# Second layer of a two-layer network on one core: the scan's products in a tile of their own, its inputs between product and sum, its spreads ahead of most decays, and group-norm statistics on ScalarE

## The chip, the cores and the metric

The kernel runs on one NeuronCore of a Trainium2 chip. The metric is the device time of one launch in microseconds. Inputs and outputs are float32, 16 images of 128 channels at 56 x 56 pixels.

## The reference

Layer 0 is a block with a 3x3 depthwise position convolution, windowed attention over the four best windows, a 5x5 depthwise convolution of the values, and an MLP. The change leaves it alone. Layer 1 is what matters here:

```python
y = conv3x3(x) + conv_b                              # 128 -> 128 channels
seq = y.reshape(B * H * W, 8, 16)                    # 8 tokens of 16 values
xz = einsum('nld,ed->nle', seq, in_proj_w); xi, z = split(xz, 2)
xc = silu(causal_conv1d(xi) + conv1d_b)              # 32 inner channels
dt, Bm, Cm = split(einsum('nld,ed->nle', xc, x_proj_w), [1, 17])
dt = softplus(dt * dt_proj_w + dt_proj_b)
a = exp(dt[..., None] * -exp(A_log))                 # decay, 32 x 16 states
b = dt[..., None] * Bm * xc[..., None]               # input
for l in range(8):                                   # the scan
    h = a[l] * h + b[l]
    y[l] = sum(h * Cm[l], axis=-1)
out = ((y + D * xc) * silu(z)) @ out_proj_w.T
x = x + silu(group_norm(out, 4 groups) * gn_w + gn_b)
```

The group norm takes mean and variance over 32 channels and all pixels of an image, so its statistics need every block of an image's output.

## The kernel before

`layer0` writes its result `x1` to HBM image by image; then `layer1` runs. Layer 1 cuts each image into 7 blocks of 448 pixels (`BLK`), and one block with its 8 tokens is a *group*: 16 x 7 = 112 groups. A group has 14 *steps*, k = 0 to 13. Steps 2m and 2m + 1 advance token m + 1, one for each half of the state (`jp`, 896 elements in each of 128 partitions). The main loop (L1284) writes the instructions out step by step and by hand, with work for the next groups between; `_chain` (L149) then pins the order of every engine to the written one. No scheduler moves anything.

In one step the engines do this, all through functions of a few lines:

- VectorE: `advance` (L999 for token 7, L1001 otherwise), the *product* of decay `a` and the state before; `complete` (L1006), the *sum* of product and input (not in steps 12 and 13, whose token 7 needs none: its product is its state); `inject` (L991), the *input* of the step four ahead, a product of the spread `x` in PSUM with the broadcast `bb`. Beside these it has `collect` (L1032, steps 3 and 12), `direct_mul` (L960, twice in step 0) and, in steps 9 and 10 of some groups, `bn_stats` (L1080).
- TensorE: `decay` (L973) for the step two ahead and `spread` (L984) for the step five ahead, each as matmuls on 32 rows; then the step's other matmuls: `gather` (L1019), the convolution of the next image (L184), `inner` (L892: the `xc` of the group after next in step 12, the gate `zs` in step 4), `direct` (L955) and `skip` (L1025) in step 13, and smaller ones.
- ScalarE: `decay_exp` (L976), the exponential of the decay in place in PSUM; then what the step's other matmuls leave to it. In steps 4 and 12 it loads the SiLU table (L146), takes two SiLUs (L893), in some groups an eighth of an earlier image's `normalise` (L1121), and loads the exponential's table again. In step 5 it has `rate_log` (L916, L917).
- GpSimd: `weigh` (L1010) in odd steps, token l = 1 to 7, the state times the broadcast `cb`. Between: `rate_sum` (four instructions, L922 to L925) after steps 6 and 8, `product` (L951) in step 10, `gated` (L1035) in steps 4 and 13, and the `store` addition (L1126) in step 2 of some groups.
- SyncE issues every DMA.

The buffers that matter: `a` has two PSUM tiles and the product is written over the decay in place, so an `a` comes free with the sum; `x` has one PSUM tile, free with the input; the states `h` have four SBUF tiles. State tiles are taken in this order: the input of step 0, 2, 4, 6, 8, 10, the product of token 7 in step 12, the input of step 12. So the input of step 12 takes the tile of token 5, which the weigh of token 5 (the one of step 9) must have read.

The names used below: A(k), I(k), S(k) are product, input and sum of step k on VectorE; w(l) is the weigh of token l on GpSimd; k over 13 means the next group.

Of the kernel before, what the change touches and what calls it, by code (L numbers as in the profile page):

```python
# [10 lines left out]
F32 = mybir.dt.float32  # L11
U32 = mybir.dt.uint32
AF = mybir.ActivationFunctionType
ALU = mybir.AluOpType
# [3 lines left out]
P = 128  # L18
H = W = 56
HW = H * W  # L20
# [3 lines left out]
BLK = 448  # L24
NBLK = HW // BLK
# [770 lines left out]
def layer1(ctx: ExitStack, tc: tile.TileContext, x1, t, out, conv):  # L796
# [15 lines left out]
    nc = tc.nc  # L812
# [3 lines left out]
    cst = ctx.enter_context(tc.tile_pool(name="l1c", bufs=1))  # L816
# [16 lines left out]
    vec = conv.vec  # L833
# [5 lines left out]


    for w, name in ((wx, "b_kx"), (wv, "b_dtw")):
        k = w1.tile(list(w.shape), F32, tag="fold", name=name)
# [6 lines left out]
    eps = cst.tile([P, 1], F32, tag="eps1", name="eps1")  # L849
    nc.vector.memset(eps, GN_EPS)  # L850
    neg = cst.tile([P, 1], F32, tag="neg", name="neg")
    nc.vector.memset(neg, -1.0)

    y, tails = conv.y, conv.tails
# [100 lines left out]
        nc.tensor.matmul(pq[0][:, 0:BLK], lhsT=cbm, rhs=p["cb"], start=True, stop=True)  # L955

    def direct_mul(p):
        ud = p["ud"] = w2.tile([P, 2, BLK], F32, tag="ud", name=f"ud_{p['n']}")
        for h in range(2):
            nc.vector.scalar_tensor_tensor(  # L960
                ud[:, h, :], pq[0][:, 0:BLK], vec[:, 6 + h : 7 + h], p["dtx"][:, h, :], ALU.mult, ALU.mult
            )


# [10 lines left out]
    def decay_exp(p, l, jp):  # L975
        nc.scalar.activation(p["a", l, jp], p["a", l, jp], AF.Exp)  # L976
# [16 lines left out]
    def advance(p, l, jp):  # L993

        a, before = p["a", l, jp], p["h", l - 1][:, own(jp), :]
        if l == 7:
            if jp == 0:
                p["h", l] = w4.tile([P, 4, BLK], F32, tag="h", name=f"h_{p['n']}_{l}")
            nc.vector.tensor_mul(p["h", l][:, own(jp), :], a, before)  # L999
        else:  # L1000
            nc.vector.tensor_mul(a, a, before)  # L1001

    def complete(p, l, jp):
        if l < 7:
            h = p["h", l][:, own(jp), :]
            nc.vector.tensor_add(h, p["a", l, jp], h)  # L1006

    def weigh(p, l):
        c = p["c", l] = w4.tile([P, 4, BLK], F32, tag="cst", name=f"cst_{p['n']}_{l}")
# [19 lines left out]
    def collect(p, h):  # L1029
        if h == 0:  # L1030
            p["ym"] = w1.tile([P, 2, BLK], F32, tag="ym", name=f"ym_{p['n']}")
        nc.vector.tensor_add(p["ym"][:, h, :], pq[1][:, 0:BLK], p["ud"][:, h, :])  # L1032

    def gated(p, h):
        nc.gpsimd.tensor_mul(p["ym"][:, h, :], p["ym"][:, h, :], p["zs"][:, h, :])  # L1035
# [1 line left out]
    xrs = {}  # L1037
# [32 lines left out]
    norms = {}  # L1070

    def statistics(b, i):
        if i == 0:
            norms[b] = (
                w2.tile([P, NBLK, 6], F32, tag="stats", name=f"stats_{b}"),
                w2.tile([P, 2], F32, tag="mv", name=f"mv_{b}"),
                w2.tile([P, 6], F32, tag="gst", name=f"gst_{b}"),
            )
        stats, mv, gst = norms[b]
        nc.vector.bn_stats(stats[:, i, :], xrs[b][:, i * BLK : (i + 1) * BLK])  # L1080
        if i == NBLK - 1:
            nc.vector.bn_aggr(mv, stats)

    def group_mean(b, bank):
        stats, mv, gst = norms[b]
        nc.tensor.matmul(pq[bank][:, 0:1], lhsT=gmask, rhs=mv[:, 0:1], start=True, stop=True)
        nc.scalar.copy(gst[:, 0:1], pq[bank][:, 0:1])

    def deviation(b):
        stats, mv, gst = norms[b]  # L1090
        nc.gpsimd.tensor_sub(gst[:, 1:2], mv[:, 0:1], gst[:, 0:1])
        nc.gpsimd.tensor_mul(gst[:, 1:2], gst[:, 1:2], gst[:, 1:2])
        nc.gpsimd.tensor_add(gst[:, 1:2], gst[:, 1:2], mv[:, 1:2])

    def group_var(b, bank):
        stats, mv, gst = norms[b]
        nc.tensor.matmul(pq[bank][:, 0:1], lhsT=gmask, rhs=gst[:, 1:2], start=True, stop=True)
        nc.scalar.activation(gst[:, 2:3], pq[bank][:, 0:1], AF.Ln, bias=eps)
        nc.scalar.activation(gst[:, 3:4], gst[:, 2:3], AF.Exp, scale=-0.5)

    def affine(b):
        stats, mv, gst = norms[b]
        nc.gpsimd.tensor_mul(gst[:, 4:5], gst[:, 3:4], gn_w)
        nc.gpsimd.tensor_mul(gst[:, 5:6], gst[:, 0:1], gst[:, 4:5])
        nc.gpsimd.tensor_sub(gst[:, 5:6], gn_b, gst[:, 5:6])
# [11 lines left out]
            nc.sync.dma_start(res[64:P, half - 64 : half], x1[b][64:P, 0:64])  # L1117

    def normalise(b, k):
        gst, xr = norms[b][2], xrs[b][:, k * half // 4 : (k + 1) * half // 4]  # L1120
        nc.scalar.activation(xr, xr, AF.Silu, bias=gst[:, 5:6], scale=gst[:, 4:5])  # L1121

    def store(b, k, q):
# [8 lines left out]

    def finish(b):

        gst = norms[b][2]
        _act_set(tc, SILU)
        for k in range(2):
            out, res = xrs[b][:, k * half : (k + 1) * half], norms[b, k]
            for q in range(2):
                part = slice(q * half // 2, (q + 1) * half // 2)  # L1140
                nc.scalar.activation(out[:, part], out[:, part], AF.Silu, bias=gst[:, 5:6], scale=gst[:, 4:5])
                nc.vector.tensor_add(res[:, part], res[:, part], out[:, part])
            at = k * half
            nc.sync.dma_start(outv[b, 0, :, at : at + half], res[0:64])
            if k == 0:
                nc.sync.dma_start(outv[b, 1, :, 64 : half + 64], res[64:P])
            else:
                nc.sync.dma_start(outv[b, 1, :, half + 64 : HW], res[64:P, 0 : half - 64])
                nc.sync.dma_start(outv[b, 1, :, 0:64], res[64:P, half - 64 : half])
# [3 lines left out]
    def work(i, k):  # L1153
# [8 lines left out]
        if prev:  # L1162
            if k == 0:
                pe += [partial(gather, prev, 5), partial(gather, prev, 6)]
            if k == 1:
                pe.append(partial(gather, prev, 7))
            if k == 3:
                dve.append(partial(collect, prev, 1))
            if k == 4:
                pool.append(partial(gated, prev, 1))  # L1170
            if k in (5, 6):
                pe.append(partial(project_out, prev, k - 5))
            b = prev["b"]
            if prev["g"] % 2 and k in (9, 10):
                dve.append(partial(statistics, b, prev["g"] - 10 + k))
            if prev["g"] == NBLK - 1:
                if k == 9:
                    dve.append(partial(statistics, b, NBLK - 1))
                if k == 12 and b < NB - 1:
                    residual(b, 0)  # L1180
        two = at(i - 2)
# [102 lines left out]
    for i in range(-2, len(groups) + 3):  # L1284
        for k in range(14):
# [64 lines left out]
```

## Time and profile before

| | |
|---|---|
| median of 3 runs | 8306.25 us (8298.19 to 8308.66) |
| profiled execution, its own time | 8305.77 us |
| its span | 8304.0 us |
| first product of layer 1 / last | 3198.2 us / 8275.8 us from the span's start |
| mean time from one group to the next | 45.35 us |
| busy in the stretch 3400 to 8000 us (of 4600) | PE 4499.84, DVE 4473.50, POOL 4189.50, ACT 3103.93 us |
| granted TensorE clock in that stretch | 0.99 |

Layer 1 takes some 5,080 us of the span. The busy time of VectorE there is 97% of the stretch; a busy share is an average, and it doesn't say which wait ends last in a group. A DVE or POOL instruction's start and duration are in the timeline view, in us; the bracket after it is how long its engine sat idle before it and what ended that. Successive VectorE instructions overlap by some 0.09 us when nothing is waited for, so what counts below is the distance from start to start, called a *slot*.

### The profile page before, as it was taken

The page shows a single profiled execution, that of the slowest core. Times are in us where ns is not written, and L with a number is a line of the kernel's source. Part 1 is how long each engine was busy: PE and PEld are TensorE (multiplying, and loading weights), DVE is VectorE, ACT ScalarE, POOL GpSimd, SP SyncE. Part 2 cuts the span into 40 slices and gives each one's busy share as a digit, 9 for nine tenths or more (in the row PEclk, how much of TensorE's full clock was granted, in tenths as well). Part 3 has the DMA queues.
Part 4 walks back from the last instruction along what each step waited for, and adds up shares of the span by engine and source line. Part 5 has one row for each costly group of instructions (what it writes and reads, how often), then busy time and mean ns, then how long its engine had stood idle before and what let it go on. Part 6 is the DMA issues. An engine that isn't in the chain of part 4 may idle for free.

```text
span 8304.0 us, 151471 instructions
## 1 busy us (share of the span) xinstructions
PE 7835.1 (94%) x52860; PEld 3329.9 (40%) x52860; DVE 7736.9 (93%) x10346; ACT 5642.6 (68%) x10579; POOL 7054.9 (85%) x5692
## 2 busy tenths in 40 slices
PE   5999999999999998999999999999999999999998
PEld 3444444444444453333333333333333333333332
DVE  7999999999999976999999999999999999999998
ACT  4777777777777755666666666666666666666665
POOL 7888788888888725899989999999999989999997
PEclk8999999999999999999999999999999999999998
DMA  3333333333333323333333334334333343334333
GB/s 65 87 86 87 85 89 87 87 87 87 87 87 87 81 79 82 87 93 102 99 92 99 96 91 105 91 97 106 83 104 100 88 105 103 86 99 108 85 93 88
DMA packets 764584, 757.87 MB, mean 91 GB/s; under 512 B 188720, under 2 KB 663984, under 8 KB 761904
## 3 DMA queue, kind: packets, MB, share of 16 engines
q1 hardware_dynamic: 763824, 748.18, 34.9%
q8 instruction: 423, 6.93, 0.4%
q14 instruction: 337, 2.76, 0.1%
HBM read 439.61 MB, written 102.76 MB: 65 GB/s over the span
## 4 chain that ended last, share of the span: by engine, by line
PE 34%; DVE 24%; POOL 24%; issue 9%; ACT 9%; DMA 1%; SPq 0%; POOLq 0%; ACTq 0%; DVEq 0%
PE a L973 7%; DVE h L991 6%; DVE a L1001 5%; POOL cst L1010 5%; PE x L984 5%; POOL xh L315 5%; PE pq L1019 5%; PE pq L892 4%; POOL e L431 4%; DVE h L1006 4%; DVE lepe L512 3%; POOL tap L313 3%; POOL dtx L925 2%; PE pq L931 2%; DVE sst L415 2%
## 5 line engine op out<-in xcount | busy, mean ns | idle before, releaser
L1010 POOL TENSOR_TENSOR cst<-h,cb 128x1792 f32<-128x1792 f32 x784 | 3130.6, 4000 | 348.9 <-DVE h L1006 291.1
L976 ACT ACTIVATE a<-a 128x896 f32<-128x896 f32 x1568 | 1415.7, 903 | 1080.2 <-PE x L984 588.0
L991 DVE TENSOR_TENSOR h<-x,bb 128x896 f32<-128x896 f32 x1568 | 1697.5, 1083 | 96.6 <-PE x L984 58.2
L512 DVE SCALAR_TENSOR_TENSOR lepe<-vpad,lep,lepe 128x448 f32<-128x448 f32 x2688 | 1718.0, 678 | 0.5
L984 PE MATMUL x<-dtx,amask 32*128 32x448 f32 x6272 | 1626.4, 595 | 49.0 <-DVE h L991 38.5
L973 PE MATMUL a<-dt,adec 32*128 32x448 f32 x6272 | 1620.2, 593 | 53.7 <-DVE h L1006 49.9
L1006 DVE TENSOR_TENSOR h<-a,h 128x896 f32<-128x896 f32 x1344 | 1463.1, 1089 | 38.1
L1001 DVE TENSOR_TENSOR a<-a,h 128x896 f32<-128x896 f32 x1344 | 1465.7, 1091 | 26.7 <-ACT a L976 25.8
L431 POOL TENSOR_SCALAR e<-e,sst,zero 128x256 f32<-128x256 f32 x1568 | 861.1, 559 | 466.6 <-DVE sst L427 417.4
L421 ACT ACTIVATE e<-ps,sst 128x256 f32<-128x256 f32 x1568 | 728.6, 469 | 522.5 <-DVE sst L415 470.5
L973 PEld LDWEIGHTS a<-dt,adec 32*128 32x128 f32 x6272 | 474.5, 185 | 1066.5 <-DVE h L1006 501.4
L315 POOL TENSOR_TENSOR xh<-xh,tap 128x448 f32<-128x448 f32 x749 | 859.6, 1148 | 43.7
L184 PE MATMUL pq<-pad,conv 128*128 128x448 f32 x1890 | 834.8, 559 | 0.0
L1019 PE MATMUL pq<-cst,sel 128*32 128x448 f32 x6272 | 734.5, 553 | 0.8 <-POOL cst L1010 0.8
L415 DVE TENSOR_REDUCE sst<-ps 128x2 f32<-128x512 f32 x784 | 540.3, 689 | 107.9 <-PE ps L409 83.0
L146 ACT ACT_TABLE_LOAD x484 | 621.0, 1283 | 9.3 <-PEq L1341 0.7
L453 PE MATMUL ptt<-ident,e 128*128 128x128 f32 x3136 | 538.6, 283 | 93.5 <-POOL e L431 76.8
L984 PEld LDWEIGHTS x<-dtx,amask 32*128 32x128 f32 x6272 | 476.7, 185 | 365.9 <-DVE h L991 344.3
L409 PE MATMUL ps<-sel,q 32*64 32x256 f32 x6272 | 537.3, 411 | 53.2 <-ACT e L421 46.9
L313 POOL TENSOR_SCALAR tap<-pad,pos,zero 128x448 f32<-128x448 f32 x749 | 546.5, 730 | 35.7
L453 PEld LDWEIGHTS ptt<-ident,e 128*128 128x128 f32 x3136 | 366.6, 141 | 417.5 <-POOL e L431 237.0
L459 ACT COPY att<-ptt 128x512 f32<-128x512 f32 x784 | 458.7, 585 | 72.0 <-PE ptt L453 64.1
(175 smaller groups left out, 12040.7 us busy)
## 6 DMA issues: line engine op xcount, KB each, us to landing
sel<-kv SPq DMA_DIRECT2D x3136, 64.0 KB
bb<-db SPq DMA_DIRECT2D x336, 448.0 KB
cb<-dc SPq DMA_DIRECT2D x336, 448.0 KB
pad<-x SPq DMA_DIRECT2D x32, 784.0 KB
x<-r SPq DMA_DIRECT2D x112, 224.0 KB
pad<-x SPq DMA_DIRECT2D x16, 1568.0 KB
db<-bs SPq DMA_DIRECT2D x112, 224.0 KB
dc<-cs SPq DMA_DIRECT2D x112, 224.0 KB
```

The costliest lines, as they stand in the source:

```text
L315: nc.gpsimd.tensor_add(im["xh"][i], im["xh"][i], held["tap"])
L431: nc.gpsimd.tensor_scalar(e, e, im["st", w][:, 2, p : p + 1], zero, ALU.mult, ALU.add)
L453: nc.tensor.transpose(ptt[:, P * (2 * p + h) : P * (2 * p + h + 1)], e[:, h * P : (h + 1) * P], ident)
L512: nc.vector.scalar_tensor_tensor(out, src, lep[:, k : k + 1], acc, ALU.mult, ALU.add)
L973: nc.tensor.matmul(a[:, k, :], lhsT=adec[rows, l4, :], rhs=p["dt"][rows, h, :], start=True, stop=True)
L976: nc.scalar.activation(p["a", l, jp], p["a", l, jp], AF.Exp)
L984: nc.tensor.matmul(x[:, k, :], lhsT=mask[rows, l4, :], rhs=p["dtx"][rows, h, :], start=True, stop=True)
L991: nc.vector.tensor_mul(p["h", l][:, own(jp), :], px["x"], weight)
L1001: nc.vector.tensor_mul(a, a, before)
L1006: nc.vector.tensor_add(h, p["a", l, jp], h)
L1010: nc.gpsimd.tensor_mul(c, p["h", l], p["gate", 1, l].unsqueeze(1).to_broadcast([P, 4, BLK]))
L1019: nc.tensor.matmul(py[32 * j : 32 * j + 32], lhsT=sel[:, l4, :], rhs=p["c", l][:, j, :], start=False, stop=(l % 4 == 3), skip_group_check= ...
```

## The change

Five edits, all in `layer1`:

1. `advance` writes the product for tokens 1 to 6 to a new SBUF tile `m`, of which there is one (`w1`, one buffer), in place of over the decay; `complete` adds from it. The setup's two `fold` tiles take the new tag.
2. The written order on VectorE: product, other work, input, sum (before: product, other work, sum, input). In step 0 the two `direct_mul` stay behind the input, so now stand between input and sum.
3. On TensorE the spread of a step stands ahead of its decay, but in steps 2, 10 and 11, where the decay stays first. The exponential follows the decay as before.
4. The group norm's statistics of a block: three ScalarE instructions with two accumulator outputs (sum; minus the block's mean; sum of squares about it) in place of `bn_stats` on VectorE, and four small ones in place of `bn_aggr` at an image's end. They stand in the same steps (9 and 10), ahead of the convolution's eviction. The scratch tile `junk` shares the tag `e` of `rate`.
5. Housekeeping for SBUF: `ud` becomes two tiles, one single and one double buffered; `eps` and `neg` share a tile.

```diff
     def direct_mul(p):
-        ud = p["ud"] = w2.tile([P, 2, BLK], F32, tag="ud", name=f"ud_{p['n']}")
         for h in range(2):
+            ud = p["ud", h] = (w1, w2)[h].tile([P, BLK], F32, tag=f"ud{h}", name=f"ud{h}_{p['n']}")
             nc.vector.scalar_tensor_tensor(
-                ud[:, h, :], pq[0][:, 0:BLK], vec[:, 6 + h : 7 + h], p["dtx"][:, h, :], ALU.mult, ALU.mult
+                ud, pq[0][:, 0:BLK], vec[:, 6 + h : 7 + h], p["dtx"][:, h, :], ALU.mult, ALU.mult
             )
...
         else:
-            nc.vector.tensor_mul(a, a, before)
+            m = p["m", l, jp] = w1.tile([P, 2, BLK], F32, tag="m", name=f"m_{p['n']}_{l}_{jp}")
+            nc.vector.tensor_mul(m, a, before)
...
             h = p["h", l][:, own(jp), :]
-            nc.vector.tensor_add(h, p["a", l, jp], h)
+            nc.vector.tensor_add(h, p["m", l, jp], h)
...
-        stats, mv, gst = norms[b]
-        nc.vector.bn_stats(stats[:, i, :], xrs[b][:, i * BLK : (i + 1) * BLK])
+        stats, gst = norms[b]
+        total, less, square = (stats[:, s, :] for s in range(3))
+        out = xrs[b][:, i * BLK : (i + 1) * BLK]
+        junk = w2.tile([P, BLK], F32, tag="e", name=f"junk_{b}_{i}")
+        nc.scalar.activation(junk, out, AF.Identity, accum_out=total[:, i : i + 1])
+        nc.scalar.activation(less[:, i : i + 1], total[:, i : i + 1], AF.Identity, scale=-1.0 / BLK)
+        nc.scalar.activation(junk, out, AF.Square, bias=less[:, i : i + 1], accum_out=square[:, i : i + 1])
         if i == NBLK - 1:
-            nc.vector.bn_aggr(mv, stats)
+            one, mean, var = junk[:, 0:NBLK], gst[:, 6:7], gst[:, 7:8]
+            nc.scalar.activation(one, total, AF.Identity, scale=1.0 / HW, accum_out=mean)
+            nc.scalar.activation(one, square, AF.Identity, scale=1.0 / HW, accum_out=gst[:, 0:1])
+            nc.scalar.activation(one, less, AF.Square, bias=mean, accum_out=gst[:, 1:2])
+            nc.scalar.activation(var, gst[:, 1:2], AF.Identity, bias=gst[:, 0:1], scale=1.0 / NBLK)
...
             if prev["g"] % 2 and k in (9, 10):
-                dve.append(partial(statistics, b, prev["g"] - 10 + k))
+                pe.append(partial(statistics, b, prev["g"] - 10 + k))
...
             for part in dve if k else ():
                 part()
-            if now:
-                complete(*state_step(i, k))
             if inputs:
                 inject(*inputs)
             for part in () if k else dve:
                 part()
-            if decays:
+            if now:
+                complete(*state_step(i, k))
+
+            apart = k in (2, 10, 11)
+            if decays and apart:
                 decay(*decays)
             if further:
                 spread(*further)
             if decays:
+                if not apart:
+                    decay(*decays)
                 decay_exp(*decays)
```

In the built program each product from step 1 to step 11 carries two waits: one for the exponential, as before, and a new one for the sum of the step before it, the last reader of the one tile `m`. The second wait stands as an instruction of its own ahead of the product. The sum waits for its own product, as before. The order on GpSimd and on the DMA queue is unchanged.

More of the change, by code (lines that the diff above doesn't have):

```diff
@@ L841, in layer1 @@
     for w, name in ((wx, "b_kx"), (wv, "b_dtw")):
-        k = w1.tile(list(w.shape), F32, tag="fold", name=name)
+        k = w1.tile(list(w.shape), F32, tag="m", name=name)
         nc.sync.dma_start(k, t[name])
@@ L848, in layer1 @@
     nc.vector.tensor_scalar_mul(dd, ident, d_w)
-    eps = cst.tile([P, 1], F32, tag="eps1", name="eps1")
+    small = cst.tile([P, 2], F32, tag="small", name="small")
+    eps, neg = small[:, 0:1], small[:, 1:2]
     nc.vector.memset(eps, GN_EPS)
-    neg = cst.tile([P, 1], F32, tag="neg", name="neg")
     nc.vector.memset(neg, -1.0)
@@ L1031, in collect @@
             p["ym"] = w1.tile([P, 2, BLK], F32, tag="ym", name=f"ym_{p['n']}")
-        nc.vector.tensor_add(p["ym"][:, h, :], pq[1][:, 0:BLK], p["ud"][:, h, :])
+        nc.vector.tensor_add(p["ym"][:, h, :], pq[1][:, 0:BLK], p["ud", h])
     def gated(p, h):
@@ L1074, in statistics @@
             norms[b] = (
-                w2.tile([P, NBLK, 6], F32, tag="stats", name=f"stats_{b}"),
-                w2.tile([P, 2], F32, tag="mv", name=f"mv_{b}"),
-                w2.tile([P, 6], F32, tag="gst", name=f"gst_{b}"),
-            )
-        stats, mv, gst = norms[b]
-        nc.vector.bn_stats(stats[:, i, :], xrs[b][:, i * BLK : (i + 1) * BLK])
-        if i == NBLK - 1:
-            nc.vector.bn_aggr(mv, stats)
+                w2.tile([P, 3, NBLK], F32, tag="stats", name=f"stats_{b}"),
@@ new lines, in statistics @@
+                w2.tile([P, 8], F32, tag="gst", name=f"gst_{b}"),
+            )
+        stats, gst = norms[b]
[5 more added lines that the diff above has]
+        nc.scalar.activation(junk, out, AF.Square, bias=less[:, i : i + 1], accum_out=square[:, i : i + 1])
@@ L1084, in group_mean @@
+        if i == NBLK - 1:
+            one, mean, var = junk[:, 0:NBLK], gst[:, 6:7], gst[:, 7:8]
[3 more added lines that the diff above has]
+            nc.scalar.activation(var, gst[:, 1:2], AF.Identity, bias=gst[:, 0:1], scale=1.0 / NBLK)
     def group_mean(b, bank):
-        stats, mv, gst = norms[b]
@@ L1086, in group_mean @@
-        nc.tensor.matmul(pq[bank][:, 0:1], lhsT=gmask, rhs=mv[:, 0:1], start=True, stop=True)
+        gst = norms[b][1]
+        nc.tensor.matmul(pq[bank][:, 0:1], lhsT=gmask, rhs=gst[:, 6:7], start=True, stop=True)
         nc.scalar.copy(gst[:, 0:1], pq[bank][:, 0:1])
     def deviation(b):
-        stats, mv, gst = norms[b]
-        nc.gpsimd.tensor_sub(gst[:, 1:2], mv[:, 0:1], gst[:, 0:1])
+        gst = norms[b][1]
+        nc.gpsimd.tensor_sub(gst[:, 1:2], gst[:, 6:7], gst[:, 0:1])
         nc.gpsimd.tensor_mul(gst[:, 1:2], gst[:, 1:2], gst[:, 1:2])
-        nc.gpsimd.tensor_add(gst[:, 1:2], gst[:, 1:2], mv[:, 1:2])
+        nc.gpsimd.tensor_add(gst[:, 1:2], gst[:, 1:2], gst[:, 7:8])
@@ L1095, in group_var @@
     def group_var(b, bank):
-        stats, mv, gst = norms[b]
+        gst = norms[b][1]
         nc.tensor.matmul(pq[bank][:, 0:1], lhsT=gmask, rhs=gst[:, 1:2], start=True, stop=True)
@@ L1101, in affine @@
     def affine(b):
-        stats, mv, gst = norms[b]
+        gst = norms[b][1]
         nc.gpsimd.tensor_mul(gst[:, 4:5], gst[:, 3:4], gn_w)
@@ L1119, in normalise @@
     def normalise(b, k):
-        gst, xr = norms[b][2], xrs[b][:, k * half // 4 : (k + 1) * half // 4]
+        gst, xr = norms[b][1], xrs[b][:, k * half // 4 : (k + 1) * half // 4]
         nc.scalar.activation(xr, xr, AF.Silu, bias=gst[:, 5:6], scale=gst[:, 4:5])
@@ L1133, in finish @@
     def finish(b):
-        gst = norms[b][2]
+        gst = norms[b][1]
         _act_set(tc, SILU)
@@ L1174, in work @@
             if prev["g"] % 2 and k in (9, 10):
-                dve.append(partial(statistics, b, prev["g"] - 10 + k))
+                pe.append(partial(statistics, b, prev["g"] - 10 + k))
             if prev["g"] == NBLK - 1:
                 if k == 9:
-                    dve.append(partial(statistics, b, NBLK - 1))
+                    pe.append(partial(statistics, b, NBLK - 1))
                 if k == 12 and b < NB - 1:
```

## The prediction

> **What bounds the kernel now.** I read the page's first part, then the chain that ended last in one stretch of layer 1, then the timelines of GpSimd and VectorE over one group. The page seems to answer at once:
>
> ```profile
> PE 7835.1 (94%) x52860; PEld 3329.9 (40%) x52860; DVE 7736.9 (93%) x10346; ACT 5642.6 (68%) x10579; POOL 7054.9 (85%) x5692
> ```
>
> In layer 1 VectorE is even 97% busy, so it looks like the bound. The chain (start, length, engine, tile, line) says something narrower:
>
> ```profile
> 5269.13 1.14 POOL u L922
> ...
> 5271.56 1.13 POOL dt L924
> ...
> 5273.91 3.96 POOL cst L1010
> 5277.87 0.02 issue
> 5277.90 1.10 DVE h L991
> 5279.04 1.02 PE x L984 x4
> 5280.06 1.70 PE pq L892 x4
> ```
>
> `rate_sum`, then w(5), release an input on VectorE: I(12), which takes the state tile that w(5) reads. From the starts of all groups I worked out I(12) minus the end of w(5): in three of four it is 33 or 34 ns, at the 75th percentile 50 ns. So I(12) starts when w(5) ends. What starts w(5)? GpSimd's timeline of the next group:
>
> ```profile
> 5300.79 4.00 POOL L1010 TENSOR_TENSOR cst<-h,cb 128x1792 f32<-128x1792 f32 x1 [1.22 <-DVE h L1006]
> 5305.68 1.14 POOL L922 TENSOR_TENSOR u<-u,e 128x448 f32<-128x448 f32 x1 [0.89 <-ACT u L916]
> ...
> 5310.42 4.01 POOL L1010 TENSOR_TENSOR cst<-h,cb 128x1792 f32<-128x1792 f32 x1
> ...
> 5319.13 4.01 POOL L1010 TENSOR_TENSOR cst<-h,cb 128x1792 f32<-128x1792 f32 x1
> ```
>
> w(3) waits for S(5). Then, but for 0.89 us until ScalarE's `u` is ready, GpSimd runs without a gap through w(3), `rate_sum`, w(4), `rate_sum`, w(5). And VectorE's timeline from I(12) on:
>
> ```profile
> 5276.72 0.61 DVE L1032 TENSOR_TENSOR ym<-pq,ud 128x448 f32<-128x448 f32 x1
> 5277.90 1.09 DVE L991 TENSOR_TENSOR h<-x,bb 128x896 f32<-128x896 f32 x1 [0.56 <-POOL cst L1010]
> 5278.90 1.08 DVE L999 TENSOR_TENSOR h<-a,h 128x896 f32<-128x896 f32 x1
> 5280.11 1.09 DVE L991 TENSOR_TENSOR h<-x,bb 128x896 f32<-128x896 f32 x1
> 5281.12 1.09 DVE L1001 TENSOR_TENSOR a<-a,h 128x896 f32<-128x896 f32 x1
> 5282.24 1.09 DVE L1006 TENSOR_TENSOR h<-a,h 128x896 f32<-128x896 f32 x1
> 5283.25 1.08 DVE L991 TENSOR_TENSOR h<-x,bb 128x896 f32<-128x896 f32 x1
> 5284.25 1.27 DVE L960 SCALAR_TENSOR_TENSOR ud<-pq,vec,dtx 128x448 f32<-128x448 f32 x2
> 5285.43 1.09 DVE L1001 TENSOR_TENSOR a<-a,h 128x896 f32<-128x896 f32 x1
> ```
>
> So a group is one turn of a ring. In this turn: w(5) and its handover 4.03 (5273.87 to 5277.90), I(12) to A(15) 7.53 (to 5285.43), A(15) to A(19) 12.91 (to 5298.34), A(19) to w(3) 2.45, w(3) to w(5) 18.34; sum 45.26. The means of all groups are 4.04, 7.76 (a few groups are late here; the median is 7.53), 12.92, 2.42 and 18.14: 45.3, against 45.35 from group to group. Between w(3) and w(5) VectorE has only some slack; elsewhere it is on the ring.
>
> **What the skill says.** The Trainium skill, "VectorE: DVE Perf Modes", section "The perf-mode tier table", gives float32 `tensor_tensor` one element per cycle with operands in SBUF or PSUM. The trace agrees: product, sum and input take 1.08 to 1.09 us, a slot of 1.00 where nothing waits, so a product in SBUF is no faster. The same page, "The DRAIN you can't avoid", says a semaphore between chained instructions costs nothing extra. Here it does: A to S, where the sum waits for its product, is a slot of 1.12 (5281.12 to 5282.24). "SBUF — State Buffer", section "Who interferes with whom", says that a DVE instruction with two SBUF inputs contends with a GpSimd instruction that reads SBUF. The new sums have two. Layer 0 disagrees: L512, with two SBUF inputs, has a median of 680 ns and a maximum of 687 from 500 to 1500 us, where GpSimd is 83% busy, against a mean of 683 for L528, which reads one input from PSUM; and GpSimd's 448-element additions take a median of 1138 ns there (L315) and in layer 1 (L922). I take no contention.
>
> **The change part by part.**
>
> *Product in its own tile, input between.* S no longer follows its product, so that wait is covered (−0.12 in ten steps; step 3 and the statistics' steps already covered it). But the one tile `m` makes A(k), k = 1 to 11, wait for S(k−1), right ahead of it, by a separate waiting instruction. Its price is in layer 0, where L516 does the same:
>
> ```profile
> 1027.43 1.86 DVE L512 SCALAR_TENSOR_TENSOR lepe<-vpad,lep,lepe 128x448 f32<-128x448 f32 x3
> 1029.40 0.62 DVE L516 TENSOR_TENSOR o<-po,lepe 128x448 f32<-128x448 f32 x1
> ```
>
> From end to start that is 0.10 us, against 0.03 in A to S. So slots are 1.00 + 1.00 + (1.09 + 0.10) = 3.19 a step, before 1.00 + 1.12 + 1.01 = 3.13. Bounds: 0 (2.99 a step) and this. I take 0.10. On the ring, A(15) to A(19) becomes 3 x 3.19 + (3.19 + 0.53 for `collect`, which hid the wait before) = 13.29 in place of 12.92: **+0.37**.
>
> *The sum comes later in its step.* S starts 1.99 after A in place of 1.12, so w(3) starts **+0.87** later after A(19). Every weigh starts later by this; the others have GpSimd work ahead of them.
>
> *I(12) to A(15).* Count from I(12). Decay now stands behind the spread in step 12: it starts at 1.14 (5279.04), where before it had started at −0.76, and the exponential follows 1.06 later, from 2.20 to 3.10. A(14) at 3.22 isn't held. But steps 12 and 13 have no sum, and I(14) now comes right behind A(14): VectorE could start it at 4.22. Its spread stands behind the four `xc` matmuls (1.70), at 3.79 as before, and an input starts 1.07 after its spread (5279.04 to 5280.11): 4.86. On ScalarE the SiLU table load runs from 3.12 to 4.40, the SiLUs to 5.05 and 5.6. `direct` needs the first one's bank: 5.1 to 5.95. The two `direct_mul` start at 6.05, S(14) at 7.23, A(15) at 8.42. The exponential of A(15) needs the table load of 1.28 back, and in four groups of seven `normalise` of 0.71 ahead of it: it ends at 7.8 or 8.5, so there A(15) is at 8.55. Mean 8.5 against 7.53: **+0.97**. Bounds: 8.05, where waits cost nothing and `normalise` is absent, and 8.6.
>
> *`u` comes in time.* L922 waits for L916 in each group, 71.2 us in 102 groups, 0.70 each. In step 4 the decay followed A(4) by 2.79 us in the mean; now it follows I(4): 1.00 + 1.14 = 2.14. So ScalarE's SiLU stretch and `u` come 0.65 earlier, w(3) ends 0.87 later, and nothing is waited for: **−0.72** with GpSimd's overlap. Bounds: −0.72 and 0.
>
> Sum: 0.37 + 0.87 + 0.97 − 0.72 = **+1.49 us a group**.
>
> *Spreads ahead of decays, elsewhere.* Together they take 0.97 us on TensorE, as at 5281.69; apart each takes that. Most blocks get shorter (step 5 from 4.0 to 3.6 us), but that lies between w(3) and I(12). VectorE's own way from A(19) to I(12) is 6 x 3.19 + 2.99 + 1.53 = 23.7 us, GpSimd's 3.31 + 17.4 + 4.03 = 24.7. So VectorE should idle some 1.1 us ahead of I(12), and whatever TensorE or VectorE save there is worth nothing. If the cover were gone, the saving would count, up to 0.5 us.
>
> *Statistics.* One `bn_stats` slot (0.53) a group leaves VectorE, in steps 9 and 10, where it is idle later anyway: nothing; uncovered it would be 0.53 x 112 = 60 us. ScalarE gets some 0.58 + 0.20 + 0.25 + 0.66 + 0.20 = 1.9 us a group: 0.58 as L912, 0.66 as L916, 0.20 for reading an accumulator as at L421, 0.25 estimated from L1098 (0.26). Behind it stand the convolution's eviction and the next exponential, due two steps later; the 1.1 us cover that. On its `junk` tile it waits for L922, long done. After the last group nothing covers it: +2 us. The smaller tiles, and queues on GpSimd and SP, which keep their order: nothing.
>
> There are 112 groups, so 111 turns: 111 x 1.49 + 2 = 167. On the profiled execution's own 8305.77, which is 0.5 from the median 8306.25, that is **8470 us**.
>
> **Rivals.**
>
> *VectorE is the bound and gets faster.* For it: 97% busy. Waits covered 10 x 0.12, statistics 0.58: −1.8 a group, some 8105 us. It needs the wait on `m` to be free, and w(5) to end before VectorE comes to I(12), so GpSimd's chain shorter by over 1.1 us. Against it: the 33 ns. Chance 0.09.
>
> *The wait on `m` costs nothing or 0.03, the ring stays.* At nothing: 0.81 − 0.43 + 0.87 − 0.72 = +0.53, 8365 us; at 0.03, 8435. For it: S is done soon. Against: 5282.24. Chance 0.20.
>
> *The ring is looser than I think, and slots alone count:* 11 x 0.19 − 10 x 0.12 − 0.58 = +0.3, some 8320 to 8340. Chance 0.05.
>
> *Sums and GpSimd lock each other out.* Ten sums of 1.09 us between w(3) and w(5) would add some 10 us a group: about 9400. Against: layer 0. Chance 0.04.
>
> **The numbers.** The likeliest, 0.62, is 8470, by itself 8430 to 8550 (upper end: `u` not recovered, +2.2 a group). The range 8350 to 8550 leaves out the first and last rival, no change, and the low edge: 0.2. A measurement tells 0.2%, 17 us, from no change. Faster 0.09, same 0.04, slower 0.87.
>
> **What would show it.** Group to group 46.8 us. L991 idle for GpSimd's cst: from 16.5 to over 100 us between 3400 and 8000. L922's wait for `u` gone. Slot S to A 1.19. A(15) about 8.5 after I(12), w(3) 3.3 after A(19). DVE busy below 97%. Wrong if I(12) doesn't start at w(5)'s end, if S to A is near 1.00, or if sums or weighs last longer.

## The result and the profile after

The kernel after takes 9722.88 us in the median (9720.94 to 9726.78, 4 runs), the kernel before 8303.99 us (8298.19 to 8308.66, 4 runs): a ratio of 1.171, 95% interval 1.1689 to 1.173, or 1419 us more. The prediction was 8470 us with a range from 8350 to 8550. Its sign was right, its size was not.

All of it is in layer 1. The first product starts at 3200.6 us from the span's start (before 3198.2), the last at 9693.1 (before 8275.8): 1415 us more between them. From one group to the next it takes 58.03 us in place of 45.34.

The page of the kernel after, its first part, the chain that ended last, and two of the costliest groups (behind the bar: busy us, mean ns of one), then the same two groups of the kernel before:

```profile
PE 8164.9 (84%) x52860; PEld 3363.4 (35%) x52860; DVE 8503.1 (87%) x10218; ACT 5850.0 (60%) x11251; POOL 7740.7 (80%) x5692
...
POOL 39%; DVE 31%; PE 16%; issue 8%; ACT 5%; DMA 0%; SPq 0%; DVEq 0%; POOLq 0%; ACTq 0%
...
L1011 POOL TENSOR_TENSOR cst<-h,cb 128x1792 f32<-128x1792 f32 x784 | 3308.2, 4225 | 1147.1 <-PE a L973 772.4
...
L1007 DVE TENSOR_TENSOR h<-m,h 128x896 f32<-128x896 f32 x1344 | 2287.5, 1702 | 0.1
```

```profile
L1010 POOL TENSOR_TENSOR cst<-h,cb 128x1792 f32<-128x1792 f32 x784 | 3130.6, 4000 | 348.9 <-DVE h L1006 291.1
...
L1006 DVE TENSOR_TENSOR h<-a,h 128x896 f32<-128x896 f32 x1344 | 1463.1, 1089 | 38.1
```

No engine is busier as a share of the span than before, but instructions have become longer, two kinds above all. The sum (L1007) took 1089 ns in the mean and takes 1702: 1344 x 0.61 = some 820 us more. The weigh (L1011) took 4000 ns and takes 4225. Both do what they did before, on as many elements. GpSimd's timeline of one group shows the lengths one by one (start, length, engine, line; the bracket is the idle time before):

```profile
6003.72 3.98 POOL L1011 TENSOR_TENSOR cst<-h,cb 128x1792 f32<-128x1792 f32 x1 [2.18 <-DVE h L1007]
6007.65 1.98 POOL L1036 TENSOR_TENSOR ym<-ym,zs 128x448 f32<-128x448 f32 x1
6012.06 3.98 POOL L1011 TENSOR_TENSOR cst<-h,cb 128x1792 f32<-128x1792 f32 x1 [2.43 <-PE a L973]
6016.01 1.98 POOL L922 TENSOR_TENSOR u<-u,e 128x448 f32<-128x448 f32 x1
6018.06 1.14 POOL L923 TENSOR_TENSOR ln<-ln,u 128x448 f32<-128x448 f32 x1
...
6022.35 4.87 POOL L1011 TENSOR_TENSOR cst<-h,cb 128x1792 f32<-128x1792 f32 x1
```

And VectorE's over the same time:

```profile
6002.47 1.08 DVE L1007 TENSOR_TENSOR h<-m,h 128x896 f32<-128x896 f32 x1
6003.65 1.09 DVE L1002 TENSOR_TENSOR m<-a,h 128x896 f32<-128x896 f32 x1
6004.66 1.08 DVE L991 TENSOR_TENSOR h<-x,bb 128x896 f32<-128x896 f32 x1
6005.66 2.98 DVE L1007 TENSOR_TENSOR h<-m,h 128x896 f32<-128x896 f32 x1
6008.75 1.09 DVE L1002 TENSOR_TENSOR m<-a,h 128x896 f32<-128x896 f32 x1
...
6022.29 1.08 DVE L1007 TENSOR_TENSOR h<-m,h 128x896 f32<-128x896 f32 x1
...
6038.42 1.09 DVE L991 TENSOR_TENSOR h<-x,bb 128x896 f32<-128x896 f32 x1 [2.33 <-POOL cst L1011]
```

Lay the two beside each other. The weigh runs from 6003.72 to 6007.70. The sum is issued at 6005.66, in the middle of it, and ends at 6008.64, 0.94 after the weigh: about what a sum takes by itself. So it did its work only after the weigh. The product and the input, at 6003.65 and 6004.66, ran beside the same weigh in their usual 1.09 and 1.08. Then the roles change: `gated` (L1036) is issued at 6007.65, while the waiting sum has its turn, and ends at 6009.63, 0.99 after the sum. The weigh at 6022.35 met a sum that was already running at 6022.29, and took 4.87. Whoever comes second waits for the other to end. In the whole trace no sum lies wholly inside a GpSimd instruction.

The page puts none of this down as idle time: a held instruction counts as busy. It shows in the mean of a group, and in the minimum, median and maximum of one line.

The means of all groups, in the prediction's own cuts of a turn:

| us | before | predicted | after |
|---|---|---|---|
| end of w(5) to I(12) | 0.07 | 0.06 | 0.12 |
| I(12) to A(15) | 7.79 | 8.73 | 11.22 |
| A(15) to A(19) | 12.92 | 13.29 | 17.09 |
| A(19) to w(3) | 2.42 | 3.29 | 3.30 |
| w(3) to the end of w(5) | 22.14 | 21.43 | 26.30 |
| sum | 45.34 | 46.80 | 58.03 |

The excess over what was predicted has three places. From w(3) to the end of w(5), +4.9: two weighs of 4.87 and 4.85 and two `rate_sum` with two held instructions each (L922 at 1.98, L924 at 1.90). From A(15) to A(19), +3.8: two sums, S(2) and S(4), held for some 1.9 each. And +2.5 from I(12) to A(15), whose one sum, S(14), is hardly ever held (1.11 us in the mean). That one is TensorE:

```profile
6039.56 1.12 PE L984 MATMUL x<-dtx,amask 32*128 32x448 f32 x2 [4.35 <-DVE h L991]
...
6041.37 3.36 PE L892 MATMUL pq<-seq,wx 128*128 128x448 f32 x4
```

After 4.35 us without work the four `xc` matmuls take 3.36 us, where the chain of the kernel before had 1.70 (+1.66), and the spread and decay ahead of them take 1.8 together in place of 0.97 (+0.85): 2.5. The clock that TensorE was granted there is half of the full one, and the slow clock is thus a second charge on top of the lock. It isn't new with this kernel: the table of half-clock groups below finds it in 16 of 100 groups of the kernel before.

### The profile page after: what moved, and what is told of

Its sections match the earlier page's. It is cut to its first block, busy times and chain, and to the rows that moved or that the text cites. A ratio compares the mean times of both kernels' runs of the same rounds, so it can differ in the third digit from the quotient of the medians.

```text
span 9723.9 us, 153470 instructions
## 1 busy us (share of the span) xinstructions
PE 8164.9 (84%) x52860; PEld 3363.4 (35%) x52860; DVE 8503.1 (87%) x10218; ACT 5850.0 (60%) x11251; POOL 7740.7 (80%) x5692
## 4 chain that ended last, share of the span: by engine, by line
POOL 39%; DVE 31%; PE 16%; issue 8%; ACT 5%; DMA 0%; SPq 0%; DVEq 0%; POOLq 0%; ACTq 0%
POOL cst L1011 14%; DVE h L1007 10%; DVE h L991 8%; PE x L984 5%; POOL xh L315 4%; POOL dt L924 4%; POOL u L922 4%; DVE m L1002 4%; PE pq L892 4%; POOL e L431 4%; POOL tap L313 3%; POOL ln L923 3%; DVE lepe L512 3%; POOL dtx L925 3%; DVE sst L415 1%
## 5 line engine op out<-in xcount | busy, mean ns | idle before, releaser
L1011 POOL TENSOR_TENSOR cst<-h,cb 128x1792 f32<-128x1792 f32 x784 | 3308.2, 4225 | 1147.1 <-PE a L973 772.4
L984 PE MATMUL x<-dtx,amask 32*128 32x448 f32 x6272 | 1883.9, 681 | 1116.2 <-DVE h L991 1102.1
L991 DVE TENSOR_TENSOR h<-x,bb 128x896 f32<-128x896 f32 x1568 | 1698.2, 1083 | 690.1 <-PE a L973 409.0
L1007 DVE TENSOR_TENSOR h<-m,h 128x896 f32<-128x896 f32 x1344 | 2287.5, 1702 | 0.1
L973 PE MATMUL a<-dt,adec 32*128 32x448 f32 x6272 | 1882.5, 681 | 41.6 <-DVE m L1002 41.6
L512 DVE SCALAR_TENSOR_TENSOR lepe<-vpad,lep,lepe 128x448 f32<-128x448 f32 x2688 | 1717.4, 677 | 0.5
L1002 DVE TENSOR_TENSOR m<-a,h 128x896 f32<-128x896 f32 x1344 | 1466.2, 1091 | 131.7 <-DVE h L1007 3.2
L984 PEld LDWEIGHTS x<-dtx,amask 32*128 32x128 f32 x6272 | 559.5, 218 | 2226.1 <-DVE h L991 1703.0
L315 POOL TENSOR_TENSOR xh<-xh,tap 128x448 f32<-128x448 f32 x749 | 858.3, 1146 | 43.7
L973 PEld LDWEIGHTS a<-dt,adec 32*128 32x128 f32 x6272 | 559.2, 218 | 282.2 <-DVE m L1002 268.9
L922 POOL TENSOR_TENSOR u<-u,e 128x448 f32<-128x448 f32 x224 | 443.2, 1978 | 75.3 <-ACT u L916 75.3
```

Of the source, the lines that this page charges most:

```text
L315: nc.gpsimd.tensor_add(im["xh"][i], im["xh"][i], held["tap"])
L512: nc.vector.scalar_tensor_tensor(out, src, lep[:, k : k + 1], acc, ALU.mult, ALU.add)
L973: nc.tensor.matmul(a[:, k, :], lhsT=adec[rows, l4, :], rhs=p["dt"][rows, h, :], start=True, stop=True)
L984: nc.tensor.matmul(x[:, k, :], lhsT=mask[rows, l4, :], rhs=p["dtx"][rows, h, :], start=True, stop=True)
L991: nc.vector.tensor_mul(p["h", l][:, own(jp), :], px["x"], weight)
L1002: nc.vector.tensor_mul(m, a, before)
```

## The experiments

The theory after the result: a sum with both inputs in SBUF and a GpSimd instruction that reads SBUF exclude each other for their whole length. Rivals: that it is this kind of instruction; that the new orders (later sums, later decays) cost most of it and long sums are only a sign; that any use of SBUF by GpSimd is enough, writes too.

**The sum as another instruction.** The kernel after with

```diff
-            nc.vector.tensor_add(h, p["m", l, jp], h)
+            nc.vector.scalar_tensor_tensor(h, p["m", l, jp], 1.0, h, ALU.mult, ALU.add)
```

> The changed kernel, but the sum is a scalar_tensor_tensor (m times 1.0, plus h) in place of a tensor_tensor: same tiles, same two SBUF inputs, same order. Theory (the instruction's kind decides: L512, a scalar_tensor_tensor with two SBUF inputs, ran 336 times wholly inside an L315 of GpSimd before, the new sum never inside a GpSimd instruction): sums go back to 1.08 us at most 1.1, weighs to 4.00, TensorE's clock to 0.98, group to group to the 46.8 us of the prediction's ring, 8470 us (8400 to 8550). Rival (any two SBUF inputs of this size exclude GpSimd): sums of up to 4.6 us stay, 9650 to 9750 us.

Measured: 9721.77 us (9720.36 to 9722.91), ratio 1.1702, 1.1684 to 1.172. Nothing changes, and the sums (minimum, median and maximum in ns) are as long as in the kernel after:

```profile
L1007 DVE SCALAR_TENSOR_TENSOR h<-m,h x1344: 1078/1082/4632, 3203.6 to 9684.9; 128x896 f32<-128x896 f32 x192
```

So the kind of instruction is not it. The run also removed the support of the prediction's argument from layer 0, whose L512 is just this kind: if it is held here and not there, something else about L512 must differ. It does (see below).

**The product in place again.** The kernel after with both new orders and the new statistics, but the product back over the decay in PSUM, so that the sum has one input in SBUF:

```diff
-            m = p["m", l, jp] = w1.tile([P, 2, BLK], F32, tag="m", name=f"m_{p['n']}_{l}_{jp}")
-            nc.vector.tensor_mul(m, a, before)
+            p["m", l, jp] = a
+            nc.vector.tensor_mul(a, a, before)
```

> The changed kernel with the product written over the decay in PSUM again; orders and statistics stay as changed. Theory (two SBUF inputs of the sum are the loss): no sum over 1.1 us, group to group 46.3 us by the ring (A(15) to A(19) 12.49, w(3) 3.3 after A(19), w(3) to w(5) 17.4 to 17.9), 8350 to 8450 us. Rival (the new orders on VectorE and TensorE starve TensorE and halve its clock): over 9000 us.

Measured: 8588.28 us (8585.26 to 8594.04), ratio 1.034, 1.0324 to 1.0355. All sums of this run, with minimum, median and maximum in ns:

```profile
L1007 DVE TENSOR_TENSOR h<-a,h x1344: 1073/1080/1093, 3201.7 to 8548.1; 128x896 f32<-128x896 f32 x192
```

Not one is held, though 544 of the 1344 lie wholly inside a weigh. So the SBUF tile `m` costs 9722.88 - 8588.28 = 1135 us of the 1419, with the half-clock groups that come with it. The other 284 are more than the prediction gave all of the orders and statistics, 167; the next runs take them apart.

**The tile with the old orders.** The kernel after with both written orders of before; own tile and statistics on ScalarE stay.

```diff
+            if now:
+                complete(*state_step(i, k))
             if inputs:
                 inject(*inputs)
...
-            if decays and apart:
+            if decays:
                 decay(*decays)
             if further:
                 spread(*further)
             if decays:
-                if not apart:
-                    decay(*decays)
                 decay_exp(*decays)
```

> The changed kernel with both written orders of the kernel before (sum ahead of the input, decay ahead of the spread); the product's own tile and the statistics on ScalarE stay. Theory (two SBUF inputs of the sum are the loss): sums up to 4.6 us and 9300 to 9800 us, whatever the order. Rival (the new orders are the loss): 8300 to 8350 us.

Measured: 9552.72 us, one run. Against the kernel with the new statistics alone (8354.67, below) the tile costs 1198 us here, against 1135 under the new orders; its sums take up to 4935 ns. The lock is there in both places of the sum in its step.

**GpSimd writes but doesn't read.** The kernel after, its weigh replaced:

```diff
-        nc.gpsimd.tensor_mul(c, p["h", l], p["gate", 1, l].unsqueeze(1).to_broadcast([P, 4, BLK]))
+        nc.gpsimd.memset(c, 0.5)
```

> The kernel after with the weigh replaced by a GpSimd memset of the same tile, so that GpSimd writes as much as before there but reads nothing, and the weigh's product is left out of what is computed. Theory: a sum with two SBUF inputs is held only by a GpSimd instruction that reads SBUF, so no sum starts or waits at the end of a memset, sums and memsets overlap freely, and what is left above 1.09 us per sum is beside rate_sum, product and gated (1.14 us each), at most some 2.2 us for a sum. Rival: any GpSimd instruction that uses SBUF holds it, writes too; then sums wait for memsets to their end, as they waited for weighs, and the memset is held by sums.

Its time (8728.58 us, one run) says nothing, since work is left out. What counts are the lengths, of sums and of memsets:

```profile
L1007 DVE TENSOR_TENSOR h<-m,h x1344: 1081/1082/1920, 3202.8 to 8694.0; 128x896 f32<-128x896 f32 x192
```

```profile
L1011 POOL MEMSET cst<- x784: 1582/1592/1608, 3191.1 to 8693.8; 128x1792 f32 x196
```

From starts and ends: 305 sums run beside a memset and no other GpSimd instruction, and take 1081 to 1092 ns; 634 us of sums and memsets overlap, and no memset is longer than 1608 ns. In one place, GpSimd:

```profile
6024.91 1.60 POOL L1011 MEMSET cst<- 128x1792 f32 x1
...
6027.69 1.13 POOL L923 TENSOR_TENSOR ln<-ln,u 128x448 f32<-128x448 f32 x1
6028.90 1.87 POOL L924 TENSOR_TENSOR dt<-dt,ln 128x448 f32<-128x448 f32 x1
```

and VectorE:

```profile
6024.98 1.08 DVE L1007 TENSOR_TENSOR h<-m,h 128x896 f32<-128x896 f32 x1
...
6028.17 1.60 DVE L1007 TENSOR_TENSOR h<-m,h 128x896 f32<-128x896 f32 x1
```

The first sum shares its whole time with a memset and is not held; the second waits for the end of L923, which reads, and then holds L924. What excludes is the reading: a GpSimd instruction that only writes, here a memset, is free. The rival falls.

**Statistics alone.** The kernel before with edit 4 alone (the ScalarE instructions in place of `bn_stats` and `bn_aggr`).

```diff
-        nc.vector.bn_stats(stats[:, i, :], xrs[b][:, i * BLK : (i + 1) * BLK])
+        nc.scalar.activation(junk, out, AF.Identity, accum_out=total[:, i : i + 1])
+        nc.scalar.activation(less[:, i : i + 1], total[:, i : i + 1], AF.Identity, scale=-1.0 / BLK)
+        nc.scalar.activation(junk, out, AF.Square, bias=less[:, i : i + 1], accum_out=square[:, i : i + 1])
...
-                dve.append(partial(statistics, b, prev["g"] - 10 + k))
+                pe.append(partial(statistics, b, prev["g"] - 10 + k))
```

> The kernel before with the statistics on ScalarE alone. The ring theory (VectorE is idle later in the same stretch, so its saved 0.53 us a group is worth nothing): ratio 0.999 to 1.001. Rival (VectorE is the bound): 0.58 x 112 = 65 us less, ratio 0.992. Third: ScalarE's 1.9 us a group delay an exponential: slower by up to 0.5%.

Measured: 8354.67 us (8349.19 to 8357.06), ratio 1.0056, 1.0042 to 1.0069: 48 us, the third of the expectations. The group takes 45.84 in place of 45.34, and the cuts place it: I(12) to A(15) 8.08 in place of 7.79, end of w(5) to I(12) 0.23 in place of 0.07, the rest unchanged within 0.06. All of it lies in the first group of each image, in whose step 9 the last block's three ScalarE instructions and the image's four stand together. There I(12) starts 1.25 after the end of w(5) (before 0.06), and A(15) comes 9.38 after I(12) (before 7.52); in the other groups both cuts are as before within 0.01. One such group, VectorE, then TensorE:

```profile
4513.41 1.09 DVE L999 TENSOR_TENSOR h<-a,h 128x896 f32<-128x896 f32 x1 [1.55 <-ACT a L976]
4514.42 0.61 DVE L1032 TENSOR_TENSOR ym<-pq,ud 128x448 f32<-128x448 f32 x1
4514.95 1.08 DVE L991 TENSOR_TENSOR h<-x,bb 128x896 f32<-128x896 f32 x1
```

```profile
4514.56 1.02 PE L973 MATMUL a<-dt,adec 32*128 32x448 f32 x4 [1.03 <-DVE h L999]
4516.09 1.06 PE L984 MATMUL x<-dtx,amask 32*128 32x448 f32 x4 [0.51 <-DVE h L991]
4517.08 3.36 PE L892 MATMUL pq<-seq,wx 128*128 128x448 f32 x4
```

A(12) waits 1.55 for its exponential, which stands behind the seven instructions and the convolution's eviction on ScalarE; so I(12), two instructions later, is late. What comes behind I(12) is something else: the four `xc` matmuls take 3.36 again, at half of TensorE's clock. The windows view shows the granted clock, 0.50, as its third number from the end:

```profile
4517.00:4520.00 3.00, 3.00 (x6) 1.18 (x4) 2.81 (x4) 1.46 (x2) 3.00 (x2) 0.50 0.02 5
```

**VectorE's order alone.** The kernel before, product in place, with

```diff
-            if now:
-                complete(*state_step(i, k))
             if inputs:
                 inject(*inputs)
             for part in () if k else dve:
                 part()
+            if now:
+                complete(*state_step(i, k))
```

> The kernel before with VectorE's new order alone: product, other work, input, sum, and in step 0 both direct_mul ahead of the sum; the product stays in place over the decay in PSUM, decays stay ahead of spreads, statistics stay on VectorE. By the ring of the prediction: A(15) to A(19) 12.9 becomes 12.5 (the sum no longer follows its product), w(3) starts 3.3 after A(19) in place of 2.4, I(12) to A(15) some 0.5 longer since direct_mul now stands ahead of S(14): +1.0 us a group, about 8415 us (8370 to 8460). Rival, that VectorE's slots count and not the ring: 10 x 0.12 less a group, about 8170.

Measured: 8563.55 us (8560.53 to 8565.16), ratio 1.0306, 1.0289 to 1.0324: 256 us, over twice the expected 107; the cuts follow below.

**Spreads ahead of decays alone.** The kernel before with

```diff
-            if decays:
+            apart = k in (2, 10, 11)
+            if decays and apart:
                 decay(*decays)
             if further:
                 spread(*further)
             if decays:
+                if not apart:
+                    decay(*decays)
                 decay_exp(*decays)
```

> The kernel before with the spread ahead of the decay in all steps but 2, 10 and 11, and nothing else. By the prediction's steps: rate_sum's wait for u (0.70 us a group) goes, worth up to 0.72; A(15) comes up to 0.97 later after I(12), since the decay of step 12 waits for I(12). Together +0.25 us a group at most, about 8330 us (8260 to 8340). Rival, that a decay behind the spread delays exponentials all along the group: A(15) to A(19) longer than 12.9 and over 8400.

Measured: 8465.57 us (8459.94 to 8471.1), ratio 1.0189, 1.0172 to 1.0206: 158 us. The cuts of the four runs without the tile ("all but the tile" is the run with the product in place again):

| us | before | statistics | order on VectorE | spread first | all but the tile |
|---|---|---|---|---|---|
| end of w(5) to I(12) | 0.07 | 0.23 | 0.80 | 0.04 | 0.99 |
| I(12) to A(15) | 7.79 | 8.08 | 8.16 | 8.69 | 9.19 |
| A(15) to A(19) | 12.92 | 12.91 | 13.44 | 12.92 | 12.58 |
| A(19) to w(3) | 2.42 | 2.42 | 3.56 | 2.42 | 3.32 |
| w(3) to the end of w(5) | 22.14 | 22.20 | 21.58 | 22.72 | 21.74 |
| sum | 45.34 | 45.84 | 47.54 | 46.80 | 47.82 |

The means mix two kinds of groups. The trace records the clock that TensorE was granted, full or half. Of 100 groups in the middle of layer 1 (numbers 5 to 104, counted from 0), those count as half-clock groups in which a half-clock stretch touches the time from I(12) to A(15):

| | before | statistics | order on VectorE | spread first | all but the tile | after |
|---|---|---|---|---|---|---|
| half-clock groups of 100 | 16 | 32 | 0 | 49 | 44 | 100 |
| I(12) to A(15) at full clock, us | 7.53 | 7.53 | 8.16 | 8.08 | 8.48 | - |
| I(12) to A(15) in half-clock groups, us | 9.12 | 9.17 | - | 9.30 | 10.18 | 11.23 |
| group at full clock, us | 45.14 | 45.06 | 47.54 | 46.15 | 47.29 | - |

So the statistics change nothing from I(12) to A(15) at full clock; they double the number of half-clock groups, and 13 of their 32 are first groups of an image, where the kernel before has none.

With the sum last, A(15) to A(19) was to shrink to 12.5 and grew to 13.44. What L991 waited for, between 3400 and 8000 us, tells why (in the kernel before the same row has 27.2 us in 42 waits):

```profile
  PE x L984: 171.3, 674
```

And what the weight loads of the decay waited for, in this run and then in the kernel before (us in total, times, longest):

```profile
PEld a L973 <- DVE h L1006: 1440.9, 1147, 2.9
```

```profile
PEld a L973 <- DVE h L1006: 434.9, 563, 1.2
```

The input now stands 1.0 us earlier in its step, and its spread comes behind a decay that needs the tile which the sum, now 0.87 later, sets free. With the spread ahead as well ("all but the tile"), the cut is 12.58. So the two orders repair each other: 256 + 158 + 48 = 462 us by themselves, 284 together. The slow clock has a share in this: none of the 256, and by the table above some 50 us of the 158 and some 40 of the 284 (an estimate: what the half-clock groups add to the mean, less the 0.20 us a group that they add before, times 111).

With the spread ahead and the sums in their old place, `u` comes later, not sooner. `rate_sum` waits for it between 3400 and 8000 us (before: 71.2 in 102):

```profile
  ACT u L916: 126.1, 99
```

The expectation had forgotten that the input, and so the spread, keeps its late place in step 4 when only TensorE's order changes; a decay behind that spread is later than before, and the SiLUs behind it too. With the sum last `u` is nearly in time: 15.7 us of waiting, and w(3) to w(5) 0.56 shorter. The other part, I(12) to A(15) +0.90, looks like the prediction's step for step 12 (+0.97), but only by luck: at full clock it is +0.55 (8.08 in place of 7.53), and the rest is that 49 groups in place of 16 are half-clock groups.

**A shorter ring.** The kernel before with one move: the second `rate_sum` behind w(5), not ahead of it.

```diff
-            if k in (6, 8):
-                pool.append(partial(rate_sum, nxt, k // 2 - 3))
+            if k in (6, 9):
+                pool.append(partial(rate_sum, nxt, k // 3 - 2))
```

> The kernel before with one edit on GpSimd: the second rate_sum (four instructions of 1.14 us) stands behind w(5) in place of ahead of it, in step 9 in place of 8. If the ring w(3), rate_sum, w(4), rate_sum, w(5), I(12) sets the time, w(5) ends up to 4.6 us earlier after w(3), I(12) no longer starts at its end, and VectorE, busy 44.1 of 45.35 us, becomes the bound: about 44.3 us a group, some 8190 us (8160 to 8260). Rival, that VectorE bounds the kernel already and the 33 ns are a coincidence: 8300, no change.

Measured: 8270.02 us (8268.88 to 8271.82), ratio 0.9955, 0.9938 to 0.9971. It is faster than both kernels, by 38 us, a third of what was expected. w(5) ends 4.5 us ahead of I(12) now, so the ring is open, but a group still takes 44.97. The windows view of 3400 to 8000 us (busy us of PE, PEld, DVE, ACT, POOL):

```profile
3400.00:8000.00 4600.00, 4515.24 (x23809) 1657.49 (x23803) 4503.36 (x4619) 3124.84 (x4375) 4219.24 (x1985) 1.00 0.37 97
```

VectorE is busy for 97.9% of it. Its 96.6 us of idle time are short waits: of sums for their products 34.8, of inputs 28.1, of products for their exponentials 33.3. So w(5) did start I(12) before, but the next limit, on VectorE's side, stood only 0.4 us a group behind it, and less than that at full clock: none of the 100 groups is a half-clock group here, and 44.97 compares with 45.14 of the kernel before. I had put VectorE at 44.1 us a group from its busy share, which leaves out these short waits.

**A mix of the orders.** To cover those waits, this move and the new orders in the steps where the run "all but the tile" had been quicker.

```diff
+            late = k in (1, 2, 4, 5, 9)
-            if now:
+            if now and not late:
                 complete(*state_step(i, k))
             if inputs:
                 inject(*inputs)
             for part in () if k else dve:
                 part()
-            if decays:
+            if now and late:
+                complete(*state_step(i, k))
+            apart = k not in (0, 1, 3, 4, 8)
+            if decays and apart:
                 decay(*decays)
             if further:
                 spread(*further)
             if decays:
+                if not apart:
+                    decay(*decays)
                 decay_exp(*decays)
```

> The kernel before with three edits: the second rate_sum behind w(5), VectorE's new order (input between product and sum) in steps 1, 2, 4, 5 and 9 alone, and the spread ahead of the decay in steps 0, 1, 3, 4 and 8 alone, the steps that feed those inputs; product in place, statistics on VectorE. From the steps of the run with all of the new orders and the product in place: such a step takes 2.99 us in place of 3.13 (steps 1, 2, 4, 5) and of 3.40 (step 9), so 0.97 us less a group, if VectorE is what bounds the kernel once w(5) is early: some 8270 - 108 = 8160 us (8130 to 8230). Rival, that a decay behind its spread or a weigh 0.87 us later is missed elsewhere in the group: 8270 or slower.

Measured: 8366.6 us (8364.43 to 8369.11), ratio 1.0074, 1.0057 to 1.0091: the rival. Steps 1 and 2 do take 2.99 us in place of 3.13, but step 4 takes 3.28, step 9 goes from 3.40 to 3.48, step 6 goes from 3.44 to 3.99 and step 0 from 4.42 to 4.95. Groups of lines between 3400 and 8000 us, here and in the run with the shorter ring alone, behind the second bar the idle time and its releasers:

```profile
L991 DVE TENSOR_TENSOR h<-x,bb 128x896 f32<-128x896 f32 x1406 | 1523.8, 1084 | 101.2 <-POOL cst L1010 54.5 <-PE a L973 17.2 <-DMA bb<-db 2.8
...
L1001 DVE TENSOR_TENSOR a<-a,h 128x896 f32<-128x896 f32 x1206 | 1316.8, 1092 | 77.1 <-ACT a L976 77.1
```

```profile
L991 DVE TENSOR_TENSOR h<-x,bb 128x896 f32<-128x896 f32 x1432 | 1549.6, 1082 | 28.1 <-POOL cst L1010 7.3 <-PE x L984 5.2 <-DMA bb<-db 2.2
...
L1001 DVE TENSOR_TENSOR a<-a,h 128x896 f32<-128x896 f32 x1229 | 1340.4, 1091 | 25.7 <-ACT a L976 25.7
```

What the sums saved is lost, as these rows show in part, in products that wait for their exponentials (25.7 to 77.1 us) and inputs that wait for weighs (7.3 to 54.5). As long as the product lies over the decay, a later sum frees the decay's tile later, two steps on.

## Why the prediction was wrong, by its steps

**The step that failed** is the last sentence on the skill: "Layer 0 disagrees: L512, with two SBUF inputs ... I take no contention." The Trainium skill, "SBUF — State Buffer", section "Who interferes with whom", had stated the rule. I set it aside for a counterexample that is none: the `lepe` accumulator that L512 reads as second input is a PSUM bank in layer 0's code (L255 takes it from the banks). The name in the profile row doesn't say where a tile lies. A line with two SBUF inputs was there, in the profile of the kernel before: L303. Beside it L512 and GpSimd's L315:

```profile
L303 DVE SCALAR_TENSOR_TENSOR xh<-pad,pos,xh x147: 668/680/1439, 19.8 to 2892.9; 128x448 f32<-128x448 f32 x147
...
L512 DVE SCALAR_TENSOR_TENSOR lepe<-vpad,lep,lepe x2688: 657/680/690, 69.8 to 3111.1; 128x448 f32<-128x448 f32 x192
...
L315 POOL TENSOR_TENSOR xh<-xh,tap x749: 1127/1138/1502, 17.7 to 2889.5; 128x448 f32<-128x448 f32 x188
```

The median of L303 is as short as L512's, but its maximum is 1439 ns where L512 has 690 over all 2688 of its instructions, and L315 goes from 1138 to 1502. I had looked at medians, and at a maximum of the wrong line. So the rival "Sums and GpSimd lock each other out" was the right one in its mechanism. Its 9400 us for 9723 came near in part by luck: it had some 10 us a group between w(3) and w(5), where 4.2 were added (26.30 for 22.14), and named nothing elsewhere, where 8.5 were: 4.2 from A(15) to A(19), whose sums are held too, 3.4 from I(12) to A(15), most of it TensorE's slow clock, and 0.9 from A(19) to w(3).

**Point by point.** *I(12) starts at w(5)'s end:* right before and after (0.12), and tested by the run that ended w(5) earlier; but VectorE, which the prediction for the changed kernel put 1.1 us behind the ring, stood at most 0.4 behind it before the change. *The wait on `m`:* right, S to A 1.18 (6002.47 to 6003.65), so 0.10 from end to start. *w(3) 3.3 after A(19):* right, 3.30. *A(15) 8.5 after I(12):* 11.22 after. Without the lock, with all orders and statistics, it is 8.48 at full clock, as predicted and by nearly the same steps (I(14) at 4.93 for 4.86, S(14) at 7.48 for 7.23), and 9.19 in the mean of all groups. *TensorE's clock:* the prediction has no term for it. Its own cut showed it, "a few groups are late here; the median is 7.53", and it didn't ask why these were late: in the kernel before they are the 16 half-clock groups. *`u` in time:* the wait is gone in the stretch 3400 to 8000 of the kernel after, but there GpSimd is late anyway; without the tile it gave 0.40, of 0.72. *Statistics at nothing:* wrong, 48 us. "Due two steps later; the 1.1 us cover that" set a mean of 1.9 us a group against the cover; at an image's end seven instructions stand together, A(12) waits 1.55 us for its exponential, and I(12) is late by 1.2. The rest is half-clock groups.

Without the tile the prediction would still have been low. For that case it had its second rival, the wait on `m` at nothing: +0.53 us a group. Measured are 47.82 - 45.34 = +2.48. Of the missing 1.95, I(12) starts 0.92 later after the end of w(5), I(12) to A(15) has 0.59 more than its share (+1.40 where the rival has 0.81; at full clock it is +0.95, the rest is more half-clock groups), `u` gives 0.32 less, and 0.12 are in the other two cuts. The largest is the step "VectorE should idle some 1.1 us ahead of I(12), and whatever TensorE or VectorE save there is worth nothing": it didn't ask whether inputs that stand earlier find their spreads ready. In steps 8 and 10 they don't: there the input starts 1.78 and 1.83 us after its product, and with nothing to wait for it would be 1.00.

What stays open: the slow clock's 2.5 us a group is read from the trace; no run kept TensorE busy to take it away. Nor do the runs show what starts a half-clock stretch where TensorE has only short pauses, as in the kernel before.

## What to carry to other kernels

Before moving an operand of a VectorE instruction from PSUM to SBUF, count its SBUF inputs: where they became two here, such an instruction and a GpSimd instruction that reads SBUF waited for one another to the end, and the price was what was left of the other instruction, not a share of its own. A counterexample to a rule needs every condition of the rule checked in the code, and the maximum of a line looked at, not its median. When one wait is found to set a period, work out how far behind the next limit stands, with the short waits of its engine and not its busy time alone. And where a mean and a median of a cut differ, split the groups by the granted clock before explaining the difference: three of the runs here had their loss in part from half-clock groups.

## What the runs showed of the hardware

- The lock of VectorE and GpSimd on reads: in the kernel after a sum of 1.08 us took up to 4.63, a GpSimd addition of 1.14 took 1.98, a weigh of 3.98 took 4.87; a GpSimd memset of 1.59 neither waited nor held. With one input in PSUM, 544 sums ran inside weighs at 1.07 to 1.09 us.
- TensorE's half speed: between 3400 and 8000 us the clock records of all these traces have full and half clock alone, and each half-clock stretch lasts 3.41 us or two or three times that. In layer 1 of the kernel after (from 3400 us on) there are 206 idle stretches of over 3.0 us, and after 200 of them the next eight matmuls have a median of over 1.0 us, mostly 1.03, where 0.59 is usual. The Trainium skill, "TensorE: Matmul & The Clock Gate", section "What's actually happening", has half the clock after an idle window of about 3.4 us. The length of the stretches agrees with such a window; that TensorE must have been idle for one does not: matmuls are as slow after 14 of 15 idle stretches of 1.75 to 2.0 us, and the kernel before, with no idle stretch of over 1.75 us between 3400 and 8000 us, has 19 half-clock stretches there, 75 us in all.
